# One-hots and row products of a graph attention layer read one operand from a PSUM bank; one exponential operation a group

## The chip, the cores and the metric

The kernel runs on one core of a Trainium2 chip. The metric is the time of one execution on the device, in microseconds (us). TensorE is called PE here, VectorE DVE, ScalarE ACT, GpSimd POOL and SyncE SP, as in the profile.

## The reference: what is computed

A graph has 12500 nodes with 128 features each and 400000 edges, sorted by target node. Two residual blocks follow one another:

```python
h = relu(layernorm(x));  x = x + rgcn2(relu(rgcn1(h)))   # 10 relations, mean per relation
h = relu(layernorm(x));  x = x + gat(h)                  # 4 heads of 32 features
# gat:
xl, xr = h @ W_l, h @ W_r
score = einsum(leaky_relu(xl[src] + xr[dst]), att)       # one value per edge and head
ex = exp(score - segment_max(score, dst)[dst])
out = segment_sum(ex / segment_sum(ex, dst)[dst] * xl[src], dst) + bias
```

The change concerns the last lines, the attention (GAT): the exponentials, and the sums over a node's edges of the exponentials and of the rows weighted by them.

## The kernel before

The edges are cut into 125 groups (G) of 3200: 128 partitions with 25 consecutive edges (J) each. Since the edges are sorted, a group covers at most 128 neighbouring nodes, and the sum over a node's edges is a matmul with a one-hot matrix: `s[p, j, n]` is 1 where edge j of partition p ends in the group's n-th node.

Three passes go over all groups, each as a software pipeline: the two relational layers (the gathers of L382) and the attention (the gathers of L365). All are written with a manual schedule: each engine does its instructions in the order of the program text, and the framework adds the semaphores between engines.

The attention stage is the loop from L894. Iteration t works on several groups at once, in this order:

- `gather` (L362 to L368): 25 indirect DMAs on POOL's queue fetch the 132-element rows of table `xl_d` for group t, each by a column of 128 indices in SBUF (`src_i`). The tile `xs` has five buffers. SP loads four small tensors for the group.
- group t-4: ACT copies the finished sums `po` from PSUM (L906).
- group t-1: ACT fills two tiles `z` in PSUM with node rows from `xn` (`first_xr`, L794).
- group t-3: `inflow` (L826): ACT copies one column to `tr` (L829), then DVE scans (L830, L835, L839), PE transposes and ACT copies `io` (L845).
- group t-1: `scores` in four parts, on DVE: a predicated copy from `xn` into `z` (L800), an addition of the gathered rows (L802), leaky ReLU times `att` (L804) and a sum over each head's features (L806). Between the parts ACT fills the third and fourth `z`.
- group t-4: `finish` (L877); group t-3: `less_maxima` (L848) subtracts the maxima from the scores `sc`.
- group t-1: `maxima` (L809), where ACT copies `sm` (L814); group t: `prepare` (L776), where PE makes `xn` (L788), one bank of PSUM with one buffer.
- group t-3: `sums` (L859), the function that is changed. In five blocks of five edges (JW), ACT writes the exponentials of a block into the last column of `xw` (L862), DVE multiplies the gathered rows by them (L863), DVE compares a row of 0 to 127 with the edges' target numbers to make the one-hots `s` (L867), and PE adds five matmuls into `po` (L871). A last matmul (L874) carries the part of a node that began in the group before. The tiles `xw` and `s` have three buffers each.

In `sums`, both operations on DVE have two inputs in SBUF: L863 the gathered rows `xs` and the exponentials in `xw`, L867 the row `iotab` (bfloat16, made from `iota` at L318) and the target numbers `dst_b`.

Of the kernel before, what the change touches and what calls it, by code (L numbers as in the profile page):

```python
# [9 lines left out]
F32 = mybir.dt.float32  # L10
I32 = mybir.dt.int32
BF16 = mybir.dt.bfloat16
AF = mybir.ActivationFunctionType
# [5 lines left out]
P = 128  # L19
J = 25  # L20
# [6 lines left out]
def kernel(  # L27
# [29 lines left out]
    nc = tc.nc  # L57
# [5 lines left out]
    H, C = att.shape  # L63
# [24 lines left out]
    iota = consts.tile([P, P], F32, name="iota")  # L88
# [212 lines left out]
    def sorted_edges():  # L301
        JW = 5
# [3 lines left out]
        with tc.tile_pool(name="sd", bufs=1, space=DRAM) as sd, tc.tile_pool(name="sk", bufs=1) as sk:  # L306
# [8 lines left out]
            pen_d = sd.tile([G, 2, P], F32, name="pen_d")  # L315
            t2v = t2_d.rearrange("(n r) d -> n (r d)", r=R)

            iotab = sk.tile([P, P], BF16, name="iotab")  # L318
            nc.vector.tensor_copy(iotab, iota)
            ecol = sk.tile([P, G], F32, name="ecol")  # L320
            nc.vector.tensor_scalar(ecol, eb, pcol, None, op0=OP.is_equal)
            prr = sk.tile([P, G], F32, name="prr")
# [50 lines left out]
            with tc.tile_pool(name="mid", bufs=1) as mid:  # L373
# [58 lines left out]
                def sums(ps, s, rs, rows):  # L432

                    for k in range(2):
                        for c in range(2):
                            a, b = s[:, 2 * k + c, :], rs[k][:, c, :]
                            if not rows:
                                a, b = b, a
                            nc.tensor.matmul(ps, a, b, start=(k == 0 and c == 0), stop=(k == 1 and c == 1),  # L439
                                             skip_group_check=True)  # L440

                def layer1():
                    with tc.tile_pool(name="fk", bufs=1) as kp, tc.tile_pool(name="fx", bufs=6) as xp, \
# [160 lines left out]
                        with tc.manual_schedule():  # L604
                            for t in range(-4, G + 3):
# [32 lines left out]
                                if 0 <= q < G:  # L638
                                    rr.append(product_sums(sp, y1, 1))
                                    pss[q] = p2.tile([P, P], F32, name="ps")  # L640
                                    sums(pss[q], ss, rr, False)
                                    xs.pop(q)

                def layer2():
                    with tc.tile_pool(name="hk", bufs=1) as kp, tc.tile_pool(name="hx", bufs=6) as xp, \
# [47 lines left out]
                        with tc.manual_schedule():  # L693
                            for t in range(G + 4):

                                if t < G:
                                    xs[t] = gather_halves(xp, t2_d[:N * R, :], idx[:, t, :])
                                q = t - 2
                                if 0 <= q < G:
                                    nodes[q] = load_node(q)  # L700
                                    sms[q] = cp.tile([P, D], F32, name="sm")
                                    nc.scalar.copy(sms[q], pss.pop(q))
                                q = t - 1
                                if 0 <= q < G:
                                    ps = pss[q] = p2.tile([P, D], F32, name="ps")
                                    ss = one_hots(sp, q)
                                    sums(ps, ss, [half_sums(yp, sp, by_slot(p2, q, k), xs[q][k], k) for k in range(2)],
                                         True)
                                    xs.pop(q)
                                    if q:  # L710

                                        nc.tensor.matmul(ps[0:1, :], ecol[:, q - 1:q], sms[q - 1],
                                                         start=False, stop=True, skip_group_check=True)
                                q = t - 2
                                if 0 <= q < G:
                                    hns[q] = node(q, sms[q], nodes[q][0])
                                q = t - 3
                                if 0 <= q < G:
                                    hTs[q] = relu_T(cp, p2, hns.pop(q))
                                q = t - 4  # L720
                                if 0 <= q < G:
                                    table(q, hTs.pop(q), nodes.pop(q)[1])
# [8 lines left out]
            with tc.tile_pool(name="gk", bufs=1) as kp, tc.tile_pool(name="gx", bufs=5) as xp, \  # L731
                    tc.tile_pool(name="gw", bufs=2) as wp, tc.tile_pool(name="gs", bufs=3) as sp, \
                    tc.tile_pool(name="gc", bufs=4) as cp, tc.tile_pool(name="gn", bufs=6) as np_, \
                    tc.tile_pool(name="gp", bufs=1, space=PSUM) as p1, \
                    tc.tile_pool(name="gp2", bufs=2, space=PSUM) as p2:
                att8 = kp.tile([P, D], F32, name="att8")
                nc.sync.dma_start(att8, att.rearrange("(o h) c -> o (h c)", o=1).to_broadcast([P, D]))
                nc.vector.tensor_scalar_mul(att8, att8, 0.8)
# [118 lines left out]
                    nc.vector.tensor_sub(sc, sc, mx)  # L857

                def sums(g, xs, sc, po, before):  # L859
                    for j0 in range(0, J, JW):  # L860
                        xw = sp.tile([P, JW, H, AW], F32, name="xw")
                        nc.scalar.activation(xw[:, :, :, C], sc[:, :, j0:j0 + JW].rearrange("p h j -> p j h"), AF.Exp)  # L862
                        nc.vector.tensor_mul(  # L863
                            xw[:, :, :, :C], xs[:, j0:j0 + JW, :D].rearrange("p j (h c) -> p j h c", h=H),
                            xw[:, :, :, C:].to_broadcast([P, JW, H, C]))
                        s = sp.tile([P, JW, P], F32, name="s")
                        nc.vector.tensor_tensor(s, iotab[:, None, :].to_broadcast([P, JW, P]),  # L867
                                                dst_b[:, g, j0:j0 + JW, None].to_broadcast([P, JW, P]),
                                                op=OP.is_equal)
                        for j in range(JW):  # L870
                            nc.tensor.matmul(po, s[:, j, :], xw[:, j].rearrange("p h a -> p (h a)"),  # L871
                                             start=(j0 + j == 0), stop=(j0 + j == J - 1), skip_group_check=True)
                    if g:
                        nc.tensor.matmul(po[0:1, :], ecol[:, g - 1:g], before, start=False, stop=True,  # L874
                                         skip_group_check=True)
# [17 lines left out]
                with tc.manual_schedule():  # L893
                    for t in range(G + 4):  # L894
# [39 lines left out]
                        if 0 <= q < G:  # L934
                            pos[q] = p1.tile([P, H * AW], F32, name="po")
                            sums(q, xs.pop(q), scs.pop(q), pos[q], sums_of.pop(q - 1, None))
# [396 lines left out]
    with tc.If(ok > 0) as cmp:  # L1333
        sorted_edges()
# [28 lines left out]
```

## Time and profile before

| | |
|---|---|
| median of 3 runs | 12567.62 us (12566.15 to 12571.2) |
| the profiled execution's own time | 12565.01 us |
| its span in the profile | 12563.2 us |
| attention stage, first gather to the end | 8370.8 to 12563.2 us |
| busy over the span: PE, DVE, ACT, POOL | 26%, 73%, 20%, 73% |
| 3125 gathers L365: busy, mean of one | 3157.4 us, 1010 ns |

The page of the profile gives the busy time of each engine, the chain of work that ended last, and the costliest groups of instructions, each with its busy time, the mean duration in ns, and the idle time of its engine just before it, with what ended that idle time. "issue" is time in which an engine waited for nothing that the profile shows. The answers about waits give the total, the number and the longest of the waits of one line for another. The timeline gives start, duration, engine, line, operation, tiles, and how many like instructions a row holds. An instruction that doesn't depend on the one before it starts up to 0.09 us before the other's recorded end, so spacing is told from start to start.

### The profile page before, as it was taken

Reading aid. Unit: us, or ns where it says so; the run is one execution under the profiler, and the core shown is the slowest. Engines: PE = TensorE matmul, PEld = TensorE weight load, DVE = VectorE, ACT = ScalarE, POOL = GpSimd, SP = SyncE. Lnnn points to the kernel's source line nnn. Section 1 sums busy time; section 2 is a strip of 40 time slices with the busy share of each in tenths; the row PEclk is TensorE's granted clock in tenths of the full one; section 3 lists DMA queues with packets and bytes.
Section 4 is the critical chain, followed back from the end, with each engine's and each line's share of the span. In section 5 each row is a group of like instructions: output and inputs, shape, how many; then the busy total and the mean of one; then the engine's idle time right before and its main releaser. Section 6 shows DMA issues by size and latency. Waiting matters only on the chain.

```text
span 12563.2 us, 69544 instructions
## 1 busy us (share of the span) xinstructions
PE 3260.9 (26%) x12778; PEld 2155.0 (17%) x12778; DVE 9221.3 (73%) x12886; ACT 2511.7 (20%) x6895; POOL 9143.9 (73%) x9384
## 2 busy tenths in 40 slices
PE   7422222222222211111111111113333333333333
PEld 3111111111111100000000000012222222232323
DVE  5777777777777666666666666668888888888888
ACT  3333333333333300000000000001111111111111
POOL 0477777777777777777777777767777777777775
PEclk9655555555555555555555555556666666666666
DMA  6433333333333222222222222222222222222222
GB/s 211 139 94 95 96 96 96 96 95 94 97 96 96 86 62 61 61 61 61 61 61 61 61 61 61 61 59 62 62 61 62 62 63 61 62 61 63 61 63 47
DMA packets 608616, 964.64 MB, mean 77 GB/s; under 512 B 193888, under 2 KB 413610, under 8 KB 608170
## 3 DMA queue, kind: packets, MB, share of 16 engines
q0 software_dynamic: 300000, 621.40, 20.5%
q1 hardware_dynamic: 278906, 267.68, 6.6%
q10 hardware_dynamic: 29264, 71.04, 1.5%
q14 instruction: 340, 2.79, 0.1%
q8 instruction: 106, 1.74, 0.1%
HBM read 758.60 MB, written 200.85 MB: 76 GB/s over the span
## 4 chain that ended last, share of the span: by engine, by line
POOL 62%; issue 24%; DVE 5%; DMA 5%; PE 3%; ACT 1%; ACTq 0%; DVEq 0%; SPq 0%; POOLq 0%
POOL xs L382 43%; POOL xs L365 20%; DMA xs<-t_d,idx 3%; PE ps L288 2%; PE po L871 1%; DMA xs<-xl_d,src_i 1%; DVE z L802 1%; DVE z L800 1%; DVE lr L804 1%; DVE sc L806 1%; DMA xt<-in_x_dram 0%; ACT z L794 0%; DVE s L867 0%; PE pa L294 0%; DVE up L760 0%
## 5 line engine op out<-in xcount | busy, mean ns | idle before, releaser
L382 POOL DMA_INDIRECT xs<-t_d,idx x6250 | 5984.6, 958 | 1941.3 <-issue 1862.7
L365 POOL DMA_INDIRECT xs<-xl_d,src_i x3125 | 3157.4, 1010 | 984.4 <-issue 931.3
L402 DVE TENSOR_TENSOR y<-xs,wk 128x3072 f32<-128x3072 f32 (+1 forms) x375 | 1324.6, 3532 | 1229.5 <-DMA xs<-t_d,idx 1215.0
L405 DVE TENSOR_REDUCE r<-y 128x256 f32<-128x3072 f32 (+1 forms) x375 | 2102.2, 5606 | 30.5 <-DVE y L402 0.9
L414 ACT ACTIVATE y<-xs,wk 128x128 f32<-128x128 f32 x3000 | 1202.6, 500 | 639.6 <-DMA xs<-t_d,idx 616.8
L439 PE MATMUL ps<-r,s 128*128 128x128 f32 x1000 | 305.5, 461 | 3390.8 <-DVE r L405 3390.8
L592 PE MATMUL pt<-wall,hT 128*128 128x512 f32 x750 | 639.2, 989 | 1533.4 <-ACT ts L594 1533.4
L871 PE MATMUL po<-xw,s 128*128 128x132 f32 x6250 | 933.2, 317 | 70.0 <-DVE s L867 60.7
L871 PEld LDWEIGHTS po<-xw,s 128*128 128x128 f32 x6250 | 896.4, 228 | 118.9 <-issue 116.8
L439 PEld LDWEIGHTS ps<-r,s 128*128 128x128 f32 x1000 | 231.9, 322 | 3517.8 <-DVE r L405 3517.8
L121 ACT ACTIVATE sd<-mv,epsc 128x1 f32<-128x1 f32 x223 | 63.6, 293 | 3549.4 <-DVE mv L119 3524.4
L820 PE MATMUL px<-ident,up 128*4 128x128 f32 x125 | 46.5, 372 | 2398.1 <-DVE up L760 2398.1
L596 DVE TENSOR_TENSOR ts<-pt,xb 128x128 f32<-128x128 f32 x125 | 36.5, 292 | 851.5 <-ACT ts L594 851.5
L863 DVE TENSOR_TENSOR xw<-xs,xw 128x640 f32<-128x640 f32 x625 | 513.2, 821 | 91.2 <-ACT xw L862 85.8
L794 ACT COPY z<-xn 128x896 f32<-128x896 f32 x500 | 397.1, 813 | 757.8 <-DVE lr L804 743.9
L802 DVE TENSOR_TENSOR z<-xs,z 128x896 f32<-128x896 f32 x500 | 498.0, 996 | 46.1 <-DMA xs<-xl_d,src_i 29.3
L592 PEld LDWEIGHTS pt<-wall,hT 128*128 128x128 f32 x750 | 210.0, 320 | 1842.5 <-ACT ts L594 1713.2
L867 DVE TENSOR_TENSOR s<-iotab,dst_b 128x640 f32<-128x640 bf16 x625 | 511.2, 818 | 0.0
L804 DVE SCALAR_TENSOR_TENSOR lr<-z,att 128x896 f32<-128x896 f32 x500 | 495.5, 991 | 17.2
L806 DVE TENSOR_REDUCE sc<-lr 128x28 f32<-128x896 f32 x500 | 494.0, 988 | 17.1
L800 DVE COPY_PREDICATED z<-mk,xn 128x896 f32<-128x896 int32 x500 | 490.3, 981 | 7.1 <-ACT z L794 7.1
L439 PE MATMUL ps<-s,r 128*128 128x128 f32 x1000 | 305.1, 461 | 644.8 <-DVE r L420 644.8
(206 smaller groups left out, 6140.6 us busy)
## 6 DMA issues: line engine op xcount, KB each, us to landing
xs<-t_d,idx POOLq DMA_INDIRECT x6250, 2.5
t_d<-ts SPq DMA_DIRECT2D x125, 640.0 KB
m<-in_edge_attr_dram SPq DMA_DIRECT2D x125, 525.0 KB
t_d<-ts ACTq DMA_DIRECT2D x98, 640.0 KB
xs<-xl_d,src_i POOLq DMA_INDIRECT x3125, 2.6
db<-drow_d SPq DMA_DIRECT2D x125, 128.0 KB
xl_d<-ts SPq DMA_DIRECT2D x125, 66.0 KB
at<-accT_d SPq DMA_DIRECT2D x125, 64.0 KB
```

Of the source, the lines that this page charges most:

```text
L365: nc.gpsimd.indirect_dma_start(out=xs[:, j, :], out_offset=None, in_=table, in_offset=bass.IndirectOffsetOnAxis(ap=ids[:, j:j + 1], axis=0))
L382: nc.gpsimd.indirect_dma_start(out=x[:, j, :], out_offset=None, in_=table, in_offset=bass.IndirectOffsetOnAxis(ap=ids[:, j0 + j:j0 + j + 1 ...
L402: nc.vector.tensor_mul(y[:, :, :n, :], xs[:, None, :n, :].to_broadcast([P, 2, n, D]), wk[:, :, :n, None].to_broadcast([P, 2, n, D]))
L405: nc.vector.tensor_reduce(r, y[:, :, :n, :].rearrange("p c j d -> p c d j"), AX.X, OP.add)
L414: nc.scalar.activation(y[:, c, :, j], xs[:, j, :], AF.Copy, scale=wk[:, c, j:j + 1])
L439: nc.tensor.matmul(ps, a, b, start=(k == 0 and c == 0), stop=(k == 1 and c == 1), skip_group_check=True)
L592: nc.tensor.matmul(pt[:, :n], hT, wall[:, c:c + n], start=True, stop=True)
L800: nc.vector.copy_predicated(z, mk[:, j0:j0 + n, None].to_broadcast([P, n, D]), xn[:, 2 * k + 1, None, :].to_broadcast([P, n, D]))
L802: nc.vector.tensor_add(z, xs[:, j0:j0 + n, :D], z)
L804: nc.vector.scalar_tensor_tensor(lr[:, :n, :], z, 0.0, att8[:, None, :].to_broadcast([P, n, D]), op0=OP.max, op1=OP.mult)
L806: nc.vector.tensor_reduce(sc[:, :, j0:j0 + n].rearrange("p h j -> p j h"), lr[:, :n, :].rearrange("p j (h c) -> p j h c", h=H), AX.X, OP.add)
L871: nc.tensor.matmul(po, s[:, j, :], xw[:, j].rearrange("p h a -> p (h a)"), start=(j0 + j == 0), stop=(j0 + j == J - 1), skip_group_check=True)
```

## The change

A tile `bank` of 512 float32 columns, one bank of PSUM, is added to the attention stage. Its first 128 columns hold the row of 0 to 127 in float32, which one DVE copy writes at the stage's start; the bfloat16 copy `iotab` is gone. Columns 128 and 256 onward hold the 100 exponentials (4 heads by 25 edges) of a group, of even and odd groups in turn.

In `sums`, one ACT operation writes all exponentials of the group into the bank. Each block then has an ACT copy from there into the last column of `xw`, where an exponential operation stood; DVE's product reads the exponentials from the bank and not from `xw`; and the one-hot comparison reads the row of 0 to 127 from the bank. The matmuls, the buffers of `xw`, `s` and `xs` and the order of everything else are as they were.

```diff
@@ -315,8 +315,6 @@
-            iotab = sk.tile([P, P], BF16, name="iotab")
-            nc.vector.tensor_copy(iotab, iota)
@@ -733,6 +731,12 @@
+                bank = p1.tile([P, 512], F32, name="bank")
+                iotap = bank[:, :P]
+                exps = [bank[:, k * P:k * P + H * J].rearrange("p (h j) -> p h j", h=H) for k in (1, 2)]
+                nc.vector.tensor_copy(iotap, iota)
@@ -857,14 +861,17 @@
                 def sums(g, xs, sc, po, before):
+                    ex = exps[g % 2]
+                    nc.scalar.activation(ex, sc, AF.Exp)
+                    ex = ex.rearrange("p h j -> p j h")
                     for j0 in range(0, J, JW):
                         xw = sp.tile([P, JW, H, AW], F32, name="xw")
-                        nc.scalar.activation(xw[:, :, :, C], sc[:, :, j0:j0 + JW].rearrange("p h j -> p j h"), AF.Exp)
+                        nc.scalar.copy(xw[:, :, :, C], ex[:, j0:j0 + JW, :])
                         nc.vector.tensor_mul(
                             xw[:, :, :, :C], xs[:, j0:j0 + JW, :D].rearrange("p j (h c) -> p j h c", h=H),
-                            xw[:, :, :, C:].to_broadcast([P, JW, H, C]))
+                            ex[:, j0:j0 + JW, :, None].to_broadcast([P, JW, H, C]))
                         s = sp.tile([P, JW, P], F32, name="s")
-                        nc.vector.tensor_tensor(s, iotab[:, None, :].to_broadcast([P, JW, P]),
+                        nc.vector.tensor_tensor(s, iotap[:, None, :].to_broadcast([P, JW, P]),
                                                 dst_b[:, g, j0:j0 + JW, None].to_broadcast([P, JW, P]),
                                                 op=OP.is_equal)
```

## The prediction

> **What bounds the kernel now.** I read the page's chain and rows first, then who waited for whom on DVE, then one round of the attention (GAT) stage in order of time. The stage runs from its first gather at 8370.8 us to the end at 12563.2; the change touches nothing else. In the page:
>
> ```profile
> POOL xs L382 43%; POOL xs L365 20%; DMA xs<-t_d,idx 3%; PE ps L288 2%; PE po L871 1%; DMA xs<-xl_d,src_i 1%; DVE z L802 1%; DVE z L800 1%; DVE lr L804 1%; DVE sc L806 1%; DMA xt<-in_x_dram 0%; ACT z L794 0%; DVE s L867 0%; PE pa L294 0%; DVE up L760 0%
> ...
> L365 POOL DMA_INDIRECT xs<-xl_d,src_i x3125 | 3157.4, 1010 | 984.4 <-issue 931.3
> ...
> L863 DVE TENSOR_TENSOR xw<-xs,xw 128x640 f32<-128x640 f32 x625 | 513.2, 821 | 91.2 <-ACT xw L862 85.8
> ...
> L867 DVE TENSOR_TENSOR s<-iotab,dst_b 128x640 f32<-128x640 bf16 x625 | 511.2, 818 | 0.0
> ```
>
> The chain puts a fifth of the span on the gathers, L365, and their row has no long idle. That invites the reading that POOL sets the stage. The waits of DVE over the whole stage contradict it (total us, times, longest):
>
> ```profile
> DVE tr L830 <- ACT tr L829: 467.3, 125, 3.8
> DVE xw L863 <- ACT xw L862: 85.8, 166, 2.0
> DVE z L802 <- DMA xs<-xl_d,src_i: 29.3, 11, 4.9
> ```
>
> DVE waited for gathered rows 11 times, 29.3 us in all, and from 8950 to 12480 not once. The last gather starts at 12479.3, yet its rows are added at about 12513. So POOL runs ahead. Gathers: (12479.3 - 8370.8) / 3124 x 25 = 32.88 us a round. DVE: the mean of 109 undisturbed rounds, from start of L830 to start of L830, is 33.17. One such round, its end:
>
> ```profile
> 10528.09 0.49 ACT L862 ACTIVATE xw<-sc 128x20 f32<-128x20 f32 x3
> 10528.36 0.83 DVE L863 TENSOR_TENSOR xw<-xs,xw 128x640 f32<-128x640 f32 x1 [0.58 <-ACT xw L862]
> 10529.10 0.82 DVE L867 TENSOR_TENSOR s<-iotab,dst_b 128x640 f32<-128x640 bf16 x1
> 10529.17 1.56 POOL L365 DMA_INDIRECT xs<-xl_d,src_i  x1 [0.30 <-issue]
> 10529.84 0.82 DVE L863 TENSOR_TENSOR xw<-xs,xw 128x640 f32<-128x640 f32 x1
> ...
> 10531.04 1.17 POOL L365 DMA_INDIRECT xs<-xl_d,src_i  x1 [0.30 <-issue]
> ...
> 10532.64 0.24 ACT L862 ACTIVATE xw<-sc 128x20 f32<-128x20 f32 x1 [4.06 <-PE po L871]
> ...
> 10535.13 0.82 DVE L867 TENSOR_TENSOR s<-iotab,dst_b 128x640 f32<-128x640 bf16 x1
> ...
> 10537.81 0.27 ACT L906 COPY su<-po 128x132 f32<-128x132 f32 x1 [3.67 <-PE po L874]
> 10537.97 1.61 ACT L794 COPY z<-xn 128x896 f32<-128x896 f32 x2
> ...
> 10539.49 0.18 ACT L829 COPY tr<-tr 4x1 f32<-4x1 f32 x1
> 10539.71 0.47 DVE L830 TENSOR_TENSOR_SCAN tr<-pen,tr,ro 4x128 f32<-4x128 f32 x1 [3.77 <-ACT tr L829]
> ```
>
> The loop is closed and has no slack: the last one-hot (L867, ends 10535.95) lets PE do five matmuls and L874; ACT then takes `po` (L906), fills two `z` (L794), copies `tr` (L829); then DVE works without a gap until L863. Whatever lengthens the five blocks L863/L867 lengthens the round.
>
> **The change part by part.**
>
> *Gathers.* 1600 gathers with no DVE operation of two SBUF inputs beside them start 1.248 us apart; 674 beside L863 or L867 start 1.514 apart (round above: 1.87 and 1.47). Taking both pairs out of that class saves 674 x 0.266 = 179 us in 116 rounds, 1.54 a round, 193 in 125. POOL's round falls to about 31.3. This lies wholly off the binding loop: POOL then meets its five buffers of `xs` and waits. The Trainium skill (SBUF — State Buffer, "Who interferes with whom") says that a DVE instruction with two SBUF inputs contends with a GpSimd instruction that reads SBUF, and that issue order decides who waits. By that, DVE could gain too. The rows decide: L863 to L867 is 0.735 us start to start at the minimum, the median and the 90th percentile, with gathers at every offset. DVE pays nothing today, so it gains 0.
>
> *DVE operands from PSUM.* Rows with 640 elements: L802 and L804, which read PSUM, 0.829 and 0.824; L863, L867 and L806 from SBUF, 0.820, 0.818, 0.822. Between nothing and +0.01 each for ten a round; I take 0.05 a round. The first copy of `iota` is once, moved from one place to another: 0.
>
> *ACT.* Five exponentials become one of 100 elements and five copies of 20. Rows of the middle rounds:
>
> ```profile
> L862 ACT ACTIVATE xw<-sc 128x20 f32<-128x20 f32 x530 | 103.0, 233 | 547.3 <-PE po L871 527.7 <-DVE xw L863 11.5 <-DVE s L867 8.0
> L814 ACT COPY sm<-sc 128x100 f32<-128x100 f32 x106 | 29.1, 274 | 1146.6 <-DVE sc L812 1146.6
> L906 ACT COPY su<-po 128x132 f32<-128x132 f32 x106 | 28.4, 268 | 394.1 <-PE po L874 394.1
> L845 ACT COPY io<-px 128x8 f32<-128x8 f32 x106 | 17.5, 165 | 151.1 <-PE px L843 151.1
> ```
>
> A copy out of PSUM: 0.165 for 8 elements, 0.268 for 132, so 0.175 for 20 (ends: 0.165, and 0.233 as the operation it replaces). The exponential: 0.274 is the SBUF copy of that size, today's exponential is some 0.03 above a copy; a PSUM destination is not in a row of that size; I take 0.28 (0.25 to 0.31). ACT is idle most of the round, so only latency counts.
>
> *A new order between ACT and DVE: the main cost.* The indices, both sets of exponentials, the copies' source and the products' source now share one bank. The skill (PSUM — Partial Sum Buffer, "PSUM bank collisions raise a hardware error") forbids two engines in one bank and quadrant at once, reads against reads included, so it wants a semaphore by bank. The trace shows how this program treats such a pair: `xn` is one bank, read by ACT (L794) and by DVE (L800). Of 500 and 500, none overlap. And in the semaphores recorded with each instruction, every second and third L800 of a round waits for ACT, the fourth never, though the fourth's `z` is filled by the last L794: the third has already waited for that read of `xn`. So reads of a bank are kept in program order. Applied here, copy k waits for one-hot k-1 on DVE, and product k for copy k. Today ACT runs three blocks ahead; afterwards it can't run ahead at all. Behind a waiting product stand, on DVE, its one-hot and then the next round; behind a waiting copy, on ACT, only the later copies and L906, which waits for PE anyway.
>
> A block: product 0.74 to the one-hot's start, one-hot 0.82, hand-over 0.03, copy 0.175, hand-over 0.03 (10528.33 to 10528.36 is one such) = 1.795, against 1.476 (0.74 + 0.735). First block: 0.28 + 0.03 + 0.175 + 0.03 = 0.515 instead of 0.27, +0.245. From the old start to the last one-hot's end: 0.245 + 4 x 1.795 + 1.56 = 8.985, and 0.05 for PSUM = 9.03. Today 7.59 in the round shown, 7.73 in the mean (some rounds lose time to PE's buffers at the fourth and fifth block, which the slower blocks absorb). Difference +1.30 a round, x 125 = +162.
>
> *What is given back.* With POOL faster and DVE slower, the early waits for gathers go, but not those before the first sums (2.83 and 1.94) and part of the next (4.9, some 2 left): 29.3 - 7 = 22. Without the new order nobody needs that cover.
>
> Sum: +162 - 22 = +140 on the profiled execution's 12565.0 (span 12563.2 and 1.8 around it) = 12705. The median of the three runs, 12567.6, lies 2.6 above the profiled one, so 12708.
>
> Own range: with the low ends a block is 1.785 and the first block's loss 0.20, +1.13 a round and all 29 given back: +112, 12680. With the high ends (copy 0.233, exponential 0.31, some 0.1 for a second semaphore on two of the copies, which also wait for PE) a block is 1.855, +1.85 a round: +231 - 18, 12780.
>
> **Rivals.**
> - *No order between reads of the bank* (the side not slower). Only the exponential must precede the product; copies run beside it. The place is L863's start; its price is +0.01 and 0.05 a round, +8, against 22 to 29 given back: 12546, within 0.2% or just past it. It decides if product k+1 starts 0.735 after one-hot k. Against it stand the 500 pairs. Chance 0.10.
> - *POOL is the bound, as the chain suggests.* Then 193 us go: 12375. It decides only where POOL's round is longer than DVE's; 32.88 against 33.17, and no wait for rows after 8950, speak against it. 0.03. That the gathers don't become faster at all would change my number by the 22 alone.
> - *PE cools.* In this round matmul records follow at 0.22 us until 10532.7, then at 0.1125. Blocks of 1.8 us leave a warm PE idle for some 0.7 each; if the clock fell to half for the last five matmuls, ten records, it adds 1.1 a round: +135, 12840. Pauses between today's blocks are too short to tell. 0.07.
> - *Order as forecast*: 12708, 0.80.
>
> **Numbers.** A difference under 0.2%, 25 us, is about what a measurement of this kernel can't tell from none. Faster: POOL's case and 0.03 of the first rival, 0.06; same: 0.07; slower: 0.87. The range 12640 to 12820 holds the likeliest case with a margin at both ends; it leaves out the first two rivals and most of the third, and keeps to 2 in 10.
>
> **What would show it.** Right: L863 waits for ACT five times a round, some 0.2 to 0.3 us each; one-hot to product start to start about 1.06 instead of 0.735; ACT's copies end their idle with L867; gathers 1.25 apart beside the sums, with POOL now idle until L863 frees `xs`; the wait L830 for L829 unchanged at 3.77. Wrong: products starting without a wait and an unchanged round of 33.17; or DVE waiting for gathers in the middle rounds; or L863 and L867 well over 0.83 with a PSUM operand; or L830's wait grown by PE.

## The result and the profile after

The changed kernel takes 12741.2 us (median of 4 runs, 12739.2 to 12755.0) against 12568.3 us before: ratio 1.0139, 95% interval 1.0124 to 1.0154. Forecast were 12708 and slower.

The profiled execution took 12755.0 us, some 14 more than the other three. Its first gather of the attention stage starts at 8383.2 us instead of 8370.8, so 12.4 us of its longer span (12753.3 against 12563.2) lie in the two stages that the change doesn't touch. The attention stage itself went from 4192.5 to 4370.1 us: +177.6. That is the number to explain.

The page of the changed kernel, chain by lines and three groups (busy, mean ns, idle before and what ended it). Line numbers have moved: L363 is the gather, L870 the product, L874 the one-hot, L865 the group's exponential, L869 ACT's copy out of the bank, L834 the scan that opens a DVE round.

```profile
POOL xs L380 42%; POOL xs L363 7%; DMA xs<-t_d,idx 3%; DVE z L806 3%; DVE lr L808 3%; DVE z L804 3%; DVE s L874 2%; DVE sc L810 2%; PE ps L288 2%; DVE xw L870 2%; DMA xs<-xl_d,src_i 2%; PE po L878 2%; ACT xw L869 1%; DVE up L764 1%; PE xn L792 0%
...
L363 POOL DMA_INDIRECT xs<-xl_d,src_i x3125 | 2970.1, 950 | 1318.5 <-issue 918.3
...
L870 DVE TENSOR_TENSOR xw<-xs,bank 128x640 f32<-128x640 f32 x625 | 513.4, 821 | 246.7 <-ACT xw L869 246.7
...
L874 DVE TENSOR_TENSOR s<-bank,dst_b 128x640 f32<-128x640 f32 x625 | 511.0, 818 | 0.0
```

The gathers got what was meant for them: 187 us less busy time. DVE was not waiting for it, and their share of the chain fell from 20% to 7%. The two DVE operations last as long as before, 821 and 818 ns. What is new is the idle time before the product.

Who waited for whom in the attention stage of the changed kernel, DVE first, then POOL (total, times, longest):

```profile
DVE tr L834 <- ACT tr L833: 467.9, 125, 3.9
DVE xw L870 <- ACT xw L869: 246.7, 625, 2.2
DVE z L806 <- DMA xs<-xl_d,src_i: 29.1, 10, 4.8
```

```profile
POOL xs L363 <- DVE xw L870: 360.6, 104, 3.6
```

Every one of the 625 products now waits for a copy. POOL waits 360.6 us for DVE to free its buffers, which it never had to do for long before. One round of the changed kernel, in order of time:

```profile
10524.65 0.24 ACT L865 ACTIVATE bank<-sc 128x100 f32<-128x100 f32 x1
10524.92 0.20 ACT L869 COPY xw<-bank 128x20 f32<-128x20 f32 x1
10525.15 0.82 DVE L870 TENSOR_TENSOR xw<-xs,bank 128x640 f32<-128x640 f32 x1 [0.76 <-ACT xw L869]
...
10525.89 0.82 DVE L874 TENSOR_TENSOR s<-bank,dst_b 128x640 f32<-128x640 f32 x1
...
10526.75 0.19 ACT L869 COPY xw<-bank 128x20 f32<-128x20 f32 x1 [1.62 <-DVE s L874]
...
10526.97 0.82 DVE L870 TENSOR_TENSOR xw<-xs,bank 128x640 f32<-128x640 f32 x1 [0.26 <-ACT xw L869]
...
10530.45 0.20 ACT L869 COPY xw<-bank 128x20 f32<-128x20 f32 x1 [1.70 <-DVE s L874]
10530.68 0.82 DVE L870 TENSOR_TENSOR xw<-xs,bank 128x640 f32<-128x640 f32 x1 [0.34 <-ACT xw L869]
...
10533.67 0.95 POOL L363 DMA_INDIRECT xs<-xl_d,src_i  x1 [3.53 <-DVE xw L870]
...
10537.90 0.47 DVE L834 TENSOR_TENSOR_SCAN tr<-pen,tr,ro 4x128 f32<-4x128 f32 x1 [3.77 <-ACT tr L833]
```

The hand-over is complete in these lines: the one-hot ends at 10526.71, the copy starts at 10526.75 and ends at 10526.94, the product starts at 10526.97. So the bank's reads alternate between the engines. The mean round of DVE is 34.58 us, from 33.17 (109 rounds each). That is 1.41 a round, or 176.5 in 125 rounds, which is nearly all of the stage's 177.6.

### The profile page after: what moved, and what is told of

Read it like the earlier page. It is cut to its first block, busy times and chain, and to the rows that moved or that the text cites. A ratio compares the mean times of both kernels' runs of the same rounds, so it can differ in the third digit from the quotient of the medians.

```text
span 12753.3 us, 69670 instructions
## 1 busy us (share of the span) xinstructions
PE 3372.8 (26%) x12778; PEld 2254.4 (18%) x12778; DVE 9240.6 (72%) x12886; ACT 2544.3 (20%) x7020; POOL 8968.0 (70%) x9384
## 4 chain that ended last, share of the span: by engine, by line
POOL 49%; issue 22%; DVE 17%; DMA 6%; PE 5%; ACT 2%; ACTq 0%; DVEq 0%; SPq 0%; POOLq 0%
POOL xs L380 42%; POOL xs L363 7%; DMA xs<-t_d,idx 3%; DVE z L806 3%; DVE lr L808 3%; DVE z L804 3%; DVE s L874 2%; DVE sc L810 2%; PE ps L288 2%; DVE xw L870 2%; DMA xs<-xl_d,src_i 2%; PE po L878 2%; ACT xw L869 1%; DVE up L764 1%; PE xn L792 0%
## 5 line engine op out<-in xcount | busy, mean ns | idle before, releaser
L363 POOL DMA_INDIRECT xs<-xl_d,src_i x3125 | 2970.1, 950 | 1318.5 <-issue 918.3
L878 PE MATMUL po<-xw,s 128*128 128x132 f32 x6250 | 1043.9, 340 | 139.4 <-DVE s L874 135.6
L878 PEld LDWEIGHTS po<-xw,s 128*128 128x128 f32 x6250 | 997.6, 249 | 197.8 <-issue 196.3
L870 DVE TENSOR_TENSOR xw<-xs,bank 128x640 f32<-128x640 f32 x625 | 513.4, 821 | 246.7 <-ACT xw L869 246.7
L806 DVE TENSOR_TENSOR z<-xs,z 128x896 f32<-128x896 f32 x500 | 497.9, 996 | 46.0 <-DMA xs<-xl_d,src_i 29.1
L874 DVE TENSOR_TENSOR s<-bank,dst_b 128x640 f32<-128x640 f32 x625 | 511.0, 818 | 0.0
```

The costliest lines, as they stand in the source:

```text
L363: nc.gpsimd.indirect_dma_start(out=xs[:, j, :], out_offset=None, in_=table, in_offset=bass.IndirectOffsetOnAxis(ap=ids[:, j:j + 1], axis=0))
L806: nc.vector.tensor_add(z, xs[:, j0:j0 + n, :D], z)
L870: nc.vector.tensor_mul(xw[:, :, :, :C], xs[:, j0:j0 + JW, :D].rearrange("p j (h c) -> p j h c", h=H), ex[:, j0:j0 + JW, :, None].to_broadc ...
```

## The experiments

Theory: DVE's loop sets the pace of the stage, and what lengthens it is that ACT's copies and DVE's reads of one bank are kept in order. Rivals: a PSUM operand slows DVE; exponential, copy and hand-over cost the same wherever the one-hots read; POOL sets the pace.

**Only the one-hots read the bank** (`e1_iota_only`). The change without its exponentials:

```diff
-                    ex = exps[g % 2]
-                    nc.scalar.activation(ex, sc, AF.Exp)
-                    ex = ex.rearrange("p h j -> p j h")
...
-                        nc.scalar.copy(xw[:, :, :, C], ex[:, j0:j0 + JW, :])
+                        nc.scalar.activation(xw[:, :, :, C], sc[:, :, j0:j0 + JW].rearrange("p h j -> p j h"), AF.Exp)
...
-                            ex[:, j0:j0 + JW, :, None].to_broadcast([P, JW, H, C]))
+                            xw[:, :, :, C:].to_broadcast([P, JW, H, C]))
```

> Only the one-hots read the bank; the exponentials are made block by block into xw, as before, so ACT never touches the bank. Theory (the order between ACT's copies and DVE's reads of one bank lengthens the DVE loop): no such order is left, the loop is 33.17 us a round as before, time 12568, within 15; one-hots stay at 0.82 us; POOL gets some 0.7 us a round faster and nobody notices. Rival 1 (a PSUM operand makes the one-hots slow): they take half of the 1.41 a round with them, time about 12655. Rival 2 (POOL sets the pace): half of its 193 us are gained, about 12470.

Measured: 12547.7 us against 12570.8 on the same chip, ratio 0.9982 (0.9975 to 0.9989). The one-hots on its page:

```profile
L871 DVE TENSOR_TENSOR s<-bank,dst_b 128x640 f32<-128x640 f32 x625 | 511.0, 818 | 0.0
```

The loss is gone whole, so the PSUM operand of the one-hots is not its cause. The gathers are busy 71 us less, and the time does not follow them down to the 12470 of the second rival. The 23 us below the kernel before were not expected; more on them below.

**Exponentials twice** (`e3_exp_twice`). DVE reads the bank as in the change; ACT only writes it, and fills `xw` from the scores. The exponentials are computed a second time:

```diff
-                        nc.scalar.copy(xw[:, :, :, C], ex[:, j0:j0 + JW, :])
+                        nc.scalar.activation(xw[:, :, :, C], sc[:, :, j0:j0 + JW].rearrange("p h j -> p j h"), AF.Exp)
```

> As the change, but ACT fills the last column of xw by exponentials of the scores in SBUF, as before, instead of copies out of the bank; so the exponentials are computed twice, and ACT only writes the bank, once a group. DVE's reads are those of the change. Theory: with no ACT read between DVE's reads no block waits; 12568 to 12591 (the latter if the first product waits for both exponentials), gathers beside the sums at 1.25 us. Rival (DVE's PSUM operands are the cost): 12741.

Measured: 12546.5 us, ratio 0.9981 (0.9973 to 0.9989). The gathers and products on its page, then POOL's wait and DVE's for the product in its stage:

```profile
L363 POOL DMA_INDIRECT xs<-xl_d,src_i x3125 | 2960.7, 947 | 1138.4 <-issue 918.2
...
L870 DVE TENSOR_TENSOR xw<-xs,bank 128x640 f32<-128x640 f32 x625 | 508.5, 814 | 84.3 <-ACT bank L865 68.8
```

```profile
POOL xs L363 <- DVE xw L870: 178.5, 92, 2.3
DVE xw L870 <- ACT bank L865: 68.8, 125, 1.8
```

This is the sharpest of the tests: the DVE operands are those of the change, the gathers are as fast as there (947 ns), and only ACT's reads of the bank are missing. The 625 waits for a copy become 125 for the one exponential, and the time is that of `e1_iota_only`. It also shows what POOL's gain is worth at most: with 197 us less of busy gathers and no new order, 24 us come out, and POOL idles 178.5 us on DVE.

**Exponentials in the bank, one-hots from SBUF** (`e2_exp_only`).

```diff
+            iotab = sk.tile([P, P], BF16, name="iotab")
+            nc.vector.tensor_copy(iotab, iota)
...
-                nc.vector.tensor_copy(iotap, iota)
...
-                        nc.vector.tensor_tensor(s, iotap[:, None, :].to_broadcast([P, JW, P]),
+                        nc.vector.tensor_tensor(s, iotab[:, None, :].to_broadcast([P, JW, P]),
```

> The exponentials of the group go to the bank and are copied to xw and read by the products from there, as in the change; the one-hots read their bfloat16 row in SBUF, as before. Theory: a copy now has to wait only for the product before it, and can run beside the one-hot, so the products again start 0.735 us after the one-hots; only the first block's exponential and copy (0.18 a round, 23 us) remain: 12591, within 15. Rival 1 (exponential, copy and hand-over cost what they cost wherever the one-hots read): about 12741. Rival 2 (POOL sets the pace): below 12568.

Measured: 12689.9 us, ratio 1.0095 (1.0079 to 1.0110): 99 us above what the theory said, and 51 below the change: a miss. A round of it:

```profile
10521.66 0.82 DVE L875 TENSOR_TENSOR s<-iotab,dst_b 128x640 f32<-128x640 bf16 x1
10521.77 0.19 ACT L870 COPY xw<-bank 128x20 f32<-128x20 f32 x1 [0.89 <-DVE xw L871]
10522.39 0.81 DVE L871 TENSOR_TENSOR xw<-xs,bank 128x640 f32<-128x640 f32 x1
...
10522.62 8.36 PE L879 MATMUL po<-xw,s 128*128 128x132 f32 x50 [0.60 <-DVE s L875]
...
10527.40 0.19 ACT L870 COPY xw<-bank 128x20 f32<-128x20 f32 x1 [2.01 <-PE po L879]
10527.62 0.82 DVE L871 TENSOR_TENSOR xw<-xs,bank 128x640 f32<-128x640 f32 x1 [0.64 <-ACT xw L870]
```

The mechanism did what was said: the copy waits for the product (L871), runs beside the one-hot, and the second and third products start 0.735 us after the one-hot before them. But the fifth waits for a copy that waits for PE. The mean of 109 rounds from the fourth one-hot to the fifth product is 1.46 us (0.91 in the kernel before), and after the last one-hot it is 0.27 us longer to the next scan. PE is slow here: its 50 records take 8.36 us instead of 7.39 in the round of before that the prediction shows. Why is told under "Not expected". Together with 0.23 at the first block, less 0.09 elsewhere, this makes the round's 34.13 - 33.17 = 0.96, x 125 = 120 us.

**Five buffers of `xw`** (`e6_xw_five`), on the changed kernel:

```diff
+                    tc.tile_pool(name="gxw", bufs=5) as xwp, \
...
-                        xw = sp.tile([P, JW, H, AW], F32, name="xw")
+                        xw = xwp.tile([P, JW, H, AW], F32, name="xw")
```

> The change with five buffers of xw instead of three, so that no copy waits for PE. In the changed kernel the products of the fourth and fifth block wait 0.337 us, the others 0.26. Theory: the 0.077 are the second semaphore of a copy that waits for PE as well as for DVE; all waits become 0.26, 0.15 a round, 19 us less: 12722. Rival (the fourth and fifth wait longer because PE is late with the matmuls): the waits stay or move to the one-hots, whose tile keeps three buffers: 12741.

Measured: 12724.9 us, ratio 1.0123 (1.0107 to 1.0138). From one-hot to product it is now 1.078 or 1.079 us at all blocks (1.077, 1.079, 1.154, 1.155 in the change), the round 34.43. So PE was not late. Of the change, where the copies of the fourth and fifth block wait for DVE and for PE, the trace has a semaphore instruction of its own ahead of each of these copies (250 of 255; the others stand before first copies; ns, min/median/max):

```profile
L869 ACTq EVENT_SEMAPHORE  x255: 17/38/38, 8482.6 to 12740.7; - x128
```

With five buffers no copy has one. The copy starts 0.111 us after the one-hot's end behind it, 0.034 without it: 0.077 us for a second semaphore, though PE had met it.

**Without the wait of 3.77 us.** To put POOL on the path, ACT's copy of the finished sums was moved behind the two `z` fills, `tr` and `io`, so that DVE's next round need not wait for PE's last block: in the changed kernel (`e4`), in the kernel before (`e5`), and in the variant with exponentials twice (`e7`).

```diff
-                        q = t - 4
-                        if 0 <= q < G:
-                            sums_of[q] = cp.tile([P, H * AW], F32, name="su")
-                            nc.scalar.copy(sums_of[q], pos.pop(q))
...
                             io, tr = inflow(q, ros, pens, tr)
+                        q = t - 4
+                        if 0 <= q < G:
+                            sums_of[q] = cp.tile([P, H * AW], F32, name="su")
+                            nc.scalar.copy(sums_of[q], pos.pop(q))
```

> The change, with ACT's copy of the finished sums (su) moved in ACT's order behind the two z fills, the tr copy and the io copy, so that DVE no longer waits 3.77 us a round for PE's last block and these copies. Theory: the DVE loop falls from 34.58 to about 30.8 us, below POOL's round of about 31.45; now POOL sets the pace, and its gain of 1.5 us a round shows: 125 x 31.45 from the first gather and some 52 us of tail, about 12355. Rival (the order within the sums costs elsewhere, or POOL is no faster when it is pressed): 12500 or more.

> The kernel before, with the same move of the su copy. Theory: the DVE loop falls to about 29.3 us, but the gathers beside the sums still take 1.5 us, so POOL's 32.9 us a round set the pace: about 12536, only 0.25% below before. The difference to the changed kernel with the same move, some 180 us, is then what the change is worth where POOL is the bound. Rival (POOL's rounds shorten as DVE has more pauses): about 12350, the same as the changed kernel with this move.

> The variant with the exponentials computed twice (no ACT read of the bank), with the same move of the su copy. Theory: POOL sets the pace here too, so the order within the sums is hidden and the time equals that of the changed kernel with the move within 15 us, about 12355, though the DVE loop is 1.4 us a round shorter. Rival (the DVE loop still decides): 175 us below the changed kernel with the move.

These fell on three other chips, on which the kernel before itself takes 14372, 14451 and 14459 us. The runs were repeated for that reason:

> The changed kernel with the su copy moved, again, since its first run was on a chip on which the kernel before took 14372 us. Theory: where the kernel before takes some 12570, the DVE loop without the 3.77 us wait is about 30.8 us, below POOL's round of 31.45; POOL sets the pace, its gain shows, about 12355. Rival (the order within the sums still decides, or POOL is no faster when it is pressed): 12500 or more.

> The kernel before with the su copy moved, again, for the same reason. Theory: the DVE loop falls to about 29.4, and POOL's 32.9 us, with the gathers slowed beside the sums, set the pace: about 12536. What the change is worth where POOL is the bound is then the difference to the changed kernel with the move, some 180. Rival (POOL's rounds shorten when DVE has pauses): about 12355.

> Exponentials computed twice, with the su copy moved, again, for the same reason. Theory: POOL sets the pace, so a DVE loop that is 1.4 us a round shorter than in the changed kernel with the move is worth nothing: within 15 us of it, about 12355. Rival (the DVE loop decides): 175 below it.

> The changed kernel with the su copy moved, a third time, in the hope of a chip on which the kernel before takes some 12570 us. Theory: with a DVE loop of about 30.8 us POOL sets the pace at 31.45 us a round, about 12355. Rival (the order within the sums still decides, or POOL is no faster when it is pressed): 12500 or more. If the kernel before takes over 14000 here too, nothing follows on POOL, and the time is within 0.4% of it.

> The kernel before with the su copy moved, beside it. Theory: POOL's 32.9 us a round set the pace, about 12536, so that the change is worth some 180 us where POOL is the bound. Rival: about 12355, no difference. If the kernel before takes over 14000 here too, nothing follows on POOL.

| ratio to the kernel before on the same chip | first chip | second | third |
|---|---|---|---|
| changed, moved (e4) | 1.0019 (1.0011 to 1.0027) | 1.0020 (1.0008 to 1.0032) | 1.0018 (1.0011 to 1.0025) |
| before, moved (e5) | 0.9989 (0.9982 to 0.9996) | 0.9991 (0.9982 to 0.9999) | 0.9988 (0.9980 to 0.9997) |
| twice, moved (e7) | 0.9954 (0.9937 to 0.9970) | 0.9964 (0.9950 to 0.9978) | not run |

The kernel before with the move, on the third chip, in order of time:

```profile
11521.46 5.13 PE L871 MATMUL po<-xw,s 128*128 128x132 f32 x30 [0.43 <-DVE s L867]
...
11533.33 0.37 ACT L862 ACTIVATE xw<-sc 128x20 f32<-128x20 f32 x2 [13.35 <-remote]
11533.60 0.83 DVE L863 TENSOR_TENSOR xw<-xs,xw 128x640 f32<-128x640 f32 x1 [9.34 <-ACT xw L862]
```

The move took the 3.77 us wait away (0.05 is left in e4, nothing in e5 and e7), but on these chips ACT's fourth exponential starts some 10 us late, and DVE with it. It waits there for PE to release its buffer, which the first block's matmuls do. In a round on the first chip the matmuls of three blocks were recorded as ended by 11508.8 us, while their three semaphore updates came together at 11515.7 to 11515.9. Rounds are 38 us there, and POOL waits for DVE's products in them (639.9 us on the third chip), so POOL was never put on the path. The times expected, 12355 and 12536 us, were not met. What the change would be worth with POOL on the path stays untested, as does the cause of the late semaphores. The chips are slow without the move too: in e5 on the first of them the attention's first gather, ahead of which the move changes nothing, starts 1121 us later than in the kernel before on the chip of the result, of some 1800 us in all. But no trace shows the unmoved attention stage on such a chip. What can be read: the variant without ACT's reads of the bank is again ahead of the change, by 84 and 79 us. That is less than the 195 of the first comparison, since the change loses less on the late fourth block (8.77 us from the third one-hot to the fourth product, against 9.55 with the exponentials twice).

## Why the prediction was right, step by step

- *What bounds the stage.* Right. DVE's loop, not the gathers. With faster gathers in every variant, POOL waited for DVE (42.5, 178.5 and 360.6 us in e1, e3 and the change) and DVE's waits for rows didn't change. POOL's rival is out.
- *A new order, block by block.* Right in mechanism, read from how the trace treats `xn`; shown by `e3_exp_twice`, which takes only ACT's reads of the bank away. Forecast for a block 1.795 us, measured 1.815 and 1.817 for the second and third (0.738 + 1.077 or 1.079): the copy takes 0.195 us, not 0.175. The fourth and fifth are 1.893: the second semaphore, which stood only in the upper end with 0.1, is real with 0.077, as the five buffers show. The four blocks so cost 0.24 a round more than forecast. First block: forecast +0.245, measured +0.23 from the exponential's start to the product's (0.50 instead of 0.27); the exponential takes 0.24, not 0.28. PSUM operands: 0.05 a round in the sum, 0 measured. Another 0.06 came back unforeseen, outside the sums (last section). In all +1.30 forecast, +1.41 measured, 14 us in 125 rounds: the sum came closer than its largest term, and that part is luck.
- *What is given back.* This term was wrong: 22 us forecast, 0 measured. The waits for rows are 29.3 us before and 29.1 after. Of the 29.3, all but 0.2 come before the stage's first product at 8472.0 us, while the pipeline fills and the first gathers arrive; I had put most of them after the sums had begun. The two misses have the same sign and come to 36 us; the measured time lies 33 above the forecast.
- *DVE pays nothing for the gathers today.* Right for L863 and L867, too broad for all of DVE; see below.
- *PE cools.* Refuted for the change: the wait for `tr` stayed 3.77. In `e2_exp_only`, where nothing was said of it, PE's clock did decide.
- The ends of the likeliest case's own range, 12680 and 12780, don't follow exactly from the terms beside them: these sum to +1.17 and +1.88 a round, so 12685 and 12785. The range on record is wider than both.

## What to carry to other kernels

Before taking contention away from an engine, look for who waits for it: a long, gapless row and a large share of the chain don't make the engine the bound, while a closed loop without slack on another one does. In this program the semaphores make engines take turns at a PSUM bank, reads included (from one-hot to product 1.08 us instead of 0.735): a constant and a value that another engine copies out had better not share a bank in an inner loop. Moving the constant out let the copies run beside the one-hots in `e2_exp_only`, though a late PE took most of the gain there. Where the value is wanted in both places, computing it twice on an idle engine (one more exponential of 0.24 us a group) was cheaper than passing it through the bank. Every bank that two engines read here is one tile, so the runs do not part an order by bank from one by tile.

## Not expected

**The clock of PE and the length of a round.** In the records of the granted clock, PE's rises to full speed lie on a fixed grid of 3.413 us in every run. In the kernel before they come 1.3 to 4.3 us after the first matmul of the sums (10th to 90th percentile), and a late rise goes with a long PE part (correlation 0.94). In `e2_exp_only` the rise comes at 5.0 to 5.1 us in nearly all rounds. The round shown above, cut at the rise (length, then busy us and count of records of PE, its weight loads, DVE, ACT and POOL, then PE's granted clock, share of DMA and GB/s):

```profile
10522.62:10527.72 5.10, 5.10 (x23) 5.10 (x24) 4.44 (x7) 0.58 (x3) 2.99 (x3) 0.50 0.23 55
10527.74:10530.98 3.24, 3.24 (x30) 3.12 (x29) 1.44 (x2) 0.00 (x0) 1.96 (x2) 1.00 0.11 25
```

So 23 matmul records touch the half clock there; in the round of before that the prediction shows it is 12, with the rise at 10532.74. The round of `e2_exp_only` is 34.06 to 34.22 us, ten windows of 3.413 being 34.13: it looks locked to the grid at a slow phase. The Trainium skill (TensorE: Matmul & The Clock Gate, "Part 1: The HAM clock gate") tells of a free-running window of 3413 ns; the grid agrees. The mean round of `e1_iota_only` and `e3_exp_twice`, 33.00 us, is 29 windows in three rounds. Why rounds lock, and why the one does so at a good phase and the other at a bad one, was not tried.

**The 23 us of e1 and e3.** Their mean rounds are 0.17 us shorter than before. Most of it is one small operation, the addition of 1e-16 to the sums (L880 before, L887 in the change), here in the kernel before and then in `e3_exp_twice` (ns, min/median/max):

```profile
L880 DVE TENSOR_SCALAR rd<-su x125: 131/346/366, 8492.7 to 12554.8; 128x4 f32<-128x4 f32 x125
```

```profile
L887 DVE TENSOR_SCALAR rd<-su x125: 131/159/377, 8496.7 to 12538.7; 128x4 f32<-128x4 f32 x125
```

In the kernel before it takes 0.159 us where the last gather began under 0.125 us ago (41 of 109 rounds) and 0.352 where it began 0.5 to 0.625 ago (68). From start to start its mean went from 0.314 us to 0.195 in e1 and 0.199 in e3, some 15 us in 125 rounds. So here a gather does seem to hold DVE up. The skill (SBUF — State Buffer, "Who interferes with whom") names `tensor_scalar` among the operations that can take the port pair shared with GpSimd. Where POOL waits for DVE's buffers (42 times in e1, 92 in e3), its gathers seem to keep a place in DVE's round, and this one is mostly harmless. That the waiting causes the place is argued from the traces, not tried by itself. In the change the operation falls as far, to 0.200, and another (L890, which divides the sums) takes 0.055 longer; so DVE's new waits cost 1.47 us a round there, of which 1.41 are left.
